# Three quads of expert weights copied during the row scatters, and a first quad of single tiles, in a two-layer mixture-of-experts kernel

## The chip, the core and the metric

The kernel runs on one core of a Trainium2 chip. A core has five engines with a queue each: TensorE (PE in the profile; PEld is its weight loading), VectorE (DVE), ScalarE (ACT), GpSimd (POOL) and SyncE (SP). [...] DMA engines move data between the on-chip memory and DRAM. The metric is the device time of one execution in microseconds.

## The reference

Two layers, each of an attention and a mixture of experts, over x of 8 sequences by 512 tokens by 128 channels. Only the last part, the experts of layer 1, is touched by the steps that follow:

```python
logits = hidden_states @ router_w + router_b
probs = softmax(logits)
topw, topi = top_k(probs, 4)                    # 4 of 16 experts for each token
topw = topw / topw.sum(-1)
combine = sum(one_hot(topi, 16) * topw[..., None], axis=2)
for each expert e:                              # w1: 128 x 256, w2: 256 x 128
    hmid = gelu(x @ w1[e] + b1[e])
    out += (hmid @ w2[e] + b2[e]) * combine[:, e]
```

4096 tokens with four experts each make 16384 assignments. All data is float32.

## The kernel before, in words

The kernel does not multiply every token by every expert. `route1(b)` finds the four experts of each token of sequence b. Its `scatter(t, rw)` then writes each token's row with its weight and its later place (130 numbers) to the DRAM tensor `rows1`, sorted by expert: 128 indirect DMAs of 128 rows (L1532), issued by POOL. While layer 1's attention and routing run, the order on the engines is found by a planner (`Order`) that holds costs and due times; it is the same in both kernels.

After this comes the stage of the expert tiles, whose order is written out by hand under `tc.manual_schedule()`. `plan()` counts the rows of each expert and divides them into tiles of 128 rows that belong to one expert; there are room and loops for 144 tiles, that is `QUADS` = 36 quads of four. For each tile it computes where the rows begin (`of_tile`), where the expert's weights begin (`off1`) and which rows aren't its own (`nowhere`). For a quad q:

- `fetch(q)` reads the four tiles of rows into `de[q]`, three DMAs on SP and one on ACT (L1690). It runs `AHEAD` = 4 quads ahead.
- `prepare(q)` transposes the four tiles on PE (L1696), copies for each tile the expert's weights from `fw1` and `fw2`, which hold all experts, to `w1_ring` and `w2_ring` on DVE (L1701, L1702), and then copies the transposed tiles to `dT` (L1703).
- `first(q)` multiplies by w1 (L1712, two products a tile, each two records in the profile) and applies gelu with the bias on ACT (L1718).
- `second(q)` multiplies by w2 (L1729), sets the places of rows that aren't the tile's own out of bounds (`to`, L1736), multiplies by the weight (y, L1737) and scatters four tiles of results to `res1` by indirect DMAs on POOL (L1739).

The loop overlaps three quads: in turn q stand `prepare(q + 1)`, `first(q)`, `fetch(q + 4)` and `second(q - 1)`. At the end the results are read back, four for each token, and added on DVE (L1772).

The on-chip memory is given out in pools. `stage.close()` releases all pools of layer 1's attention and routing together (`work1`, `small1`, `psum1`), and `work2` with all rings of the expert tiles takes their place. In `work1` lie the tiles of attention as well as `rows`, from which the row scatters read.

Of the kernel before, what the change touches and what calls it, by code (L numbers as in the profile page):

```python
# [9 lines left out]
F32 = mybir.dt.float32  # L10
I32 = mybir.dt.int32
# [3 lines left out]
ALU = mybir.AluOpType  # L15
AX = mybir.AxisListType

P = 128
B = 8
S = 512  # L20
NT = S // P
C = 128
# [15 lines left out]
I1 = 256  # L38
NC1 = I1 // P
WE = I1 + NC1  # L40

W1 = C + 2
WEIGHT, DEST = C, C + 1
REGION = B * S
NA = B * S * K1
QUADS = -(-(NA + E1 * (P - 1)) // (4 * P))
# [143 lines left out]
def two_layers(ctx: ExitStack, tc: tile.TileContext, a: dict, out: bass.AP):  # L190
    nc = tc.nc

    const = ctx.enter_context(tc.tile_pool(name="const", bufs=1))
# [4 lines left out]
    stage = ExitStack()  # L198
    const0 = stage.enter_context(tc.tile_pool(name="const0", bufs=1))

    def ring(pool, n, shape, name, dtype=F32):
        return Ring([pool.tile(shape, dtype, tag=f"{name}{i}", bufs=1, name=f"{name}{i}") for i in range(n)])

    def ring_of(pool, n, shape, name, dtype=F32):
        return [pool.tile(shape, dtype, tag=f"{name}{i}", bufs=1, name=f"{name}{i}") for i in range(n)]
# [19 lines left out]
    ident = const.tile([P, P], F32, name="ident")  # L225
# [61 lines left out]
    work = stage.enter_context(tc.tile_pool(name="work0", bufs=1))  # L287
    small = stage.enter_context(tc.tile_pool(name="small0", bufs=1))
    stage_psum = stage.enter_context(tc.tile_pool(name="psum0", bufs=1, space=bass.MemoryType.PSUM))
    tokens, columns = [P, NT, C], [P, S]  # L290
# [37 lines left out]
    zeros = const.tile([P, S], F32, name="zeros")  # L328
# [35 lines left out]
    v_ring = ring(work, 3, columns, "vT")  # L364
# [73 lines left out]
    def tiled(t2):  # L438
        return t2.rearrange("p (t c) -> p t c", t=NT)
# [20 lines left out]
    def statistics(first, last):  # L460

        yield landing(3.0 + first)
        for b in range(first, last):
            yield DVE, 1.5
            for t in range(NT):
                nc.vector.bn_stats(st_a[:, t, :], xs[b][:, t, :])
                nc.vector.bn_aggr(mv_a[:, b, t, :], st_a[:, t, :])
        yield ACT, 0.6, EXP
        rs, sh = rs_a[:, first:last, :], sh_a[:, first:last, :]
        inverse_root(rs, mv_a[:, first:last, :, 1], bias=eps)  # L470
        yield DVE, 0.2
        nc.vector.scalar_tensor_tensor(sh, mv_a[:, first:last, :, 0], -1.0, rs, ALU.mult, ALU.mult)
        for b in range(first, last):
            have_stats[b].set(order.now)
# [494 lines left out]
    work = stage.enter_context(tc.tile_pool(name="work_e", bufs=1))  # L969
# [63 lines left out]
        nc.scalar.preload_act_table_set(EXP)  # L1033

    stage.close()
    work = stage.enter_context(tc.tile_pool(name="work1", bufs=1))
    small = stage.enter_context(tc.tile_pool(name="small1", bufs=1))


    ng = NH * DK  # L1040
    full = [P, NT, K1, E1]
    ys_ring = ring(work, 2, [P, NT, 2, C], "ys")
    u_ring = ring(work, 4, tokens, "u")
    hn_ring = ring(work, 2, tokens, "hn")
    h1_ring = ring(work, 2, columns, "h1T")
    v_ring = ring(work, 3, columns, "vT")
    gk_ring = ring(work, 2, [ng, S], "gk")
    kq_ring = ring(work, 2, columns, "kq")
    za_ring = ring(work, 2, [ng, S], "za")
    gate_ring = ring(work, 3, columns, "gate")  # L1050

    four = [P, DK, S]
    kb_ring = ring(work, 3, four, "kb")
    gb_both = experts.tile([P, 2, DK, S], F32, tag="first", name="gb_both")
    qb_both = experts.tile([P, 2, DK, S], F32, tag="second", name="qb_both")
    gb_ring = Ring([gb_both[:, i] for i in range(2)])
# [4 lines left out]
    y_ring = ring(work, 2, columns, "yT")  # L1061
# [523 lines left out]
    fw1, fw2 = late  # L1585

    stage.close()
    work = ctx.enter_context(tc.tile_pool(name="work2", bufs=2))


    de_ring = ring_of(work, 8, [P, 4, W1], "de")
    to_ring = ring_of(work, 4, [P, 4], "to", I32)
    w1_ring = ring_of(work, 3, [P, 4, WE], "qw1")
    w2_ring = ring_of(work, 4, [P, 4, I1], "qw2")
    dT_ring = ring_of(work, 3, [P, S], "dT")
    hT_ring = ring_of(work, 3, [P, NC1, S], "qh")
    y_ring = ring_of(work, 4, [P, 4, C], "qy")
    yk_ring = ring_of(work, B, [P, NT, K1, C], "yk")
    psum2 = ctx.enter_context(tc.tile_pool(name="psum2", bufs=1, space=bass.MemoryType.PSUM))
    qT_banks = ring_of(psum2, 2, [P, S], "qT")  # L1600
    mid_banks = ring_of(psum2, 4, [P, S], "mid")
    qy_banks = ring_of(psum2, 2, [P, S], "qyp")
# [14 lines left out]
    nowhere = const.tile([P, 4 * QUADS], I32, name="nowhere")  # L1617
    de, hot_w, cold = {}, {}, {}
# [60 lines left out]
    def value(src, engine, low, high):  # L1679
        return nc.values_load(  # L1680
            src, engines=[engine], min_val=low, max_val=high, skip_runtime_bounds_check_because="clamped in plan()"
        )

    def fetch(q):

        de[q] = de_ring[q % len(de_ring)]
        for engine, queue, tiles_of in ((ET.SP, nc.sync, range(3)), (ET.Activation, nc.scalar, range(3, 4))):
            at = [value(of_tile[0:1, 1, 4 * q + i : 4 * q + i + 1], engine, 0, E1 * REGION - P) for i in tiles_of]
            for i in tiles_of:
                queue.dma_start(de[q][:, i, :], rows1[bass.ds(at[i - tiles_of[0]], P), :])  # L1690

    def prepare(q):

        ps = qT_banks[q % 2]
        for i in range(4):
            nc.tensor.transpose(ps[:, i * P : (i + 1) * P], de[q][:, i, 0:C], ident)  # L1696
        w1_q, w2_q, dT = w1_ring[q % 3], w2_ring[q % 4], dT_ring[q % 3]
        for i in range(4):
            n = 4 * q + i
            at = value(off1[0:1, n : n + 1], ET.DVE, 0, (E1 - 1) * WE)  # L1700
            nc.vector.tensor_copy(w1_q[:, i, :], fw1[:, bass.ds(at, WE)])  # L1701
            nc.vector.tensor_copy(w2_q[:, i, :], fw2[:, bass.ds(at, I1)])  # L1702
        nc.vector.tensor_copy(dT, ps)  # L1703

    def first(q):

        w1_q, dT, hT = w1_ring[q % 3], dT_ring[q % 3], hT_ring[q % 3]
        mid = mid_banks[2 * (q % 2) : 2 * (q % 2) + 2]
        for i in range(4):
            here = slice(i * P, (i + 1) * P)  # L1710
            for c in range(NC1):
                nc.tensor.matmul(  # L1712
                    mid[c][:, here], lhsT=w1_q[:, i, c * P : (c + 1) * P], rhs=dT[:, here], start=True, stop=True
                )
        for i in range(4):
            here = slice(i * P, (i + 1) * P)
            for c in range(NC1):
                nc.scalar.activation(  # L1718
                    hT[:, c, here], mid[c][:, here], AF.Gelu, bias=w1_q[:, i, I1 + c : I1 + c + 1]
                )  # L1720

    def second(q):

        w2_q, hT, to, y = w2_ring[q % 4], hT_ring[q % 3], to_ring[q % 4], y_ring[q % 4]
        ps = qy_banks[q % 2]
        for i in range(4):
            here = slice(i * P, (i + 1) * P)
            for c in range(NC1):
                nc.tensor.matmul(  # L1729
                    ps[:, here],  # L1730
                    lhsT=hT[:, c, here],
                    rhs=w2_q[:, i, c * C : (c + 1) * C],
                    start=c == 0,
                    stop=c == NC1 - 1,
                )
        nc.vector.tensor_tensor(to, de[q][:, :, DEST].bitcast(I32), nowhere[:, 4 * q : 4 * q + 4], ALU.max)  # L1736
        nc.vector.tensor_mul(y, tiled(ps), de[q][:, :, WEIGHT : WEIGHT + 1].to_broadcast([P, 4, C]))  # L1737
        for i in range(4):
            nc.gpsimd.indirect_dma_start(  # L1739
                out=res1_w[4 * q + i],  # L1740
                out_offset=bass.IndirectOffsetOnAxis(ap=to[:, i : i + 1], axis=0),
                in_=y[:, i, :],
                in_offset=None,
                bounds_check=NA - 1,
                oob_is_err=False,
            )

    AHEAD = 4
    with tc.manual_schedule():
        plan()  # L1750
        for q in range(AHEAD):
            fetch(q)
        prepare(0)
        for q in range(QUADS + 1):
            if q + 1 < QUADS:
                prepare(q + 1)
            if q < QUADS:
                first(q)
            if q + AHEAD < QUADS:
                fetch(q + AHEAD)  # L1760
            if q > 0:
                second(q - 1)


        for b in range(B):
            nc.sync.dma_start(
                yk_ring[b].rearrange("p t k c -> p (t k c)"),
                res1[b * S * K1 : (b + 1) * S * K1, :].rearrange("(p n) c -> p (n c)", p=P),
            )
        for b in range(B):  # L1770
            for k in range(K1):
                nc.vector.tensor_add(xs[b], xs[b], yk_ring[b][:, :, k, :])  # L1772
            nc.scalar.dma_start(out[b].rearrange("(t p) c -> p t c", p=P), xs[b])
# [37 lines left out]
```

## Time and profile before

| | us |
|---|---|
| median of three runs | 1123.48 |
| lowest and highest run | 1116.67, 1125.98 |
| the profiled execution's own time | 1110.57 |
| its span, first to last instruction | 1108.8 |
| last row scatter issued (L1532) | 826.0 |
| first, last result scatter issued (L1739) | 844.6, 1075.0 |

The profile is of one execution. Its times are counted from its first instruction. Busy time of the engines over the span: PE 831.4 us (75%), DVE 624.4 (56%), ACT 473.0 (43%), POOL 453.6 (41%). The granted TensorE clock is 0.823 of full speed in the mean; in a stretch it is a mean of pieces at 1.0 and at 0.5. In a timeline row the columns are: start, length, engine, source line, operation, what it writes and reads (buffer numbers left out), how often, and in brackets the idle time of the engine before it with what ended it. "issue" there means that the profile shows nothing that it waited for. In a row of windows they are: the stretch, its length, then busy time and count for PE, PEld, DVE, ACT and POOL, the granted clock, the busy share of the DMA engines and GB/s. In a row of the costliest groups: busy time in all and mean ns of one, then the idle time before them with its main releaser.

### The profile page before, as it was taken

To read this page: it belongs to the slowest core of one execution; us is meant where nothing else is said; L and a number is where in the kernel's file an instruction comes from. 1 tells how busy PE (TensorE), PEld (TensorE's weight loads), DVE (VectorE), ACT (ScalarE), POOL (GpSimd) and SP (SyncE) were. 2 spreads that over 40 slices of the span, in tenths; PEclk is the share of its full clock that TensorE was granted. 3 is DMA by queue.
4 is the path that set the end of the run, shared out by engine and by line. 5 is a ranking of instruction groups with operands and counts; after the bars stand their busy time and mean duration, and the time that the engine had idled before them with its cause. 6 is when DMAs were issued, how large, how long until landed. Compare 5 with 4: busy or idle time off the path is not lost. (4 is left out here: it accounts for less than half of the span.)

```text
span 1108.8 us, 13427 instructions
## 1 busy us (share of the span) xinstructions
PE 831.4 (75%) x3819; PEld 547.1 (49%) x3819; DVE 624.4 (56%) x1592; ACT 473.0 (43%) x1040; POOL 453.6 (41%) x466
## 2 busy tenths in 40 slices
PE   6888998996889299696799687675728677777730
PEld 3544465553445144233476434454418677677630
DVE  5499988778693111255866466362435445455417
ACT  6544656451624044285466654444413233243220
POOL 6200005307454335200035538585553656566650
PEclk9888889869788599898898878686758889988965
DMA  7986667464244300269741065552114232223119
GB/s 177 221 237 146 151 141 193 103 160 109 74 97 147 76 9 20 95 179 233 176 121 46 32 167 155 147 156 73 37 51 106 79 82 82 74 80 87 48 34 357
DMA packets 75531, 131.93 MB, mean 119 GB/s; under 512 B 13044, under 2 KB 54902, under 8 KB 67264
## 3 DMA queue, kind: packets, MB, share of 16 engines
q1 hardware_dynamic: 46400, 91.12, 32.3%
q0 software_dynamic: 14832, 27.84, 8.5%
q10 hardware_dynamic: 14224, 12.11, 3.7%
q8 instruction: 30, 0.49, 0.2%
q14 instruction: 45, 0.37, 0.1%
HBM read 94.79 MB, written 41.14 MB: 123 GB/s over the span
## 5 line engine op out<-in xcount | busy, mean ns | idle before, releaser
L1532 POOL DMA_INDIRECT rows<-rows,si x128 | 152.3, 1190 | 211.6 <-DVE tmp L1502 116.1
L1739 POOL DMA_INDIRECT res<-qy,to x144 | 143.3, 995 | 105.7 <-DVE qw L1701 65.6
L876 POOL DMA_INDIRECT row<-rows,si x64 | 90.1, 1408 | 226.0 <-DVE qT L587 113.7
L1718 ACT ACTIVATE qh<-mid,qw 128x128 f32<-128x128 f32 x288 | 78.7, 391 | 173.3 <-remote 90.8
L1712 PE MATMUL mid<-dT,qw 128*128 128x128 f32 x576 | 89.7, 308 | 39.0 <-issue 23.5
L1712 PEld LDWEIGHTS mid<-dT,qw 128*128 128x128 f32 x576 | 80.7, 218 | 47.9 <-issue 30.7
L671 PE MATMUL acc<-add,center 128*128 128x512 f32 x128 | 76.1, 750 | 16.6 <-DVE add L700 14.4
L1729 PE MATMUL qyp<-qw,qh 128*128 128x128 f32 x576 | 78.6, 294 | 1.6 <-issue 1.5
L1729 PEld LDWEIGHTS qyp<-qw,qh 128*128 128x128 f32 x576 | 75.8, 212 | 1.4 <-issue 1.3
L694 DVE TENSOR_TENSOR_SCAN add<-dec,add 128x2048 f32<-128x2048 f32 x16 | 70.8, 4425 | 0.7
L1737 DVE TENSOR_TENSOR qy<-qyp,de 128x512 f32<-128x512 f32 x36 | 24.8, 688 | 80.3 <-remote 44.9
L179 ACT ACT_TABLE_LOAD x48 | 61.6, 1283 | 5.2 <-issue 3.2
L1701 DVE COPY qw<-fw 128x258 f32 x144 | 43.6, 303 | 28.6 <-issue 12.0
L671 PEld LDWEIGHTS acc<-add,center 128*128 128x128 f32 x128 | 29.7, 243 | 60.0 <-issue 33.8
L1012 POOL DMA_INDIRECT res<-y,de x32 | 31.4, 980 | 46.5 <-DVE dT L985 21.9
L1696 PE MATMUL qT<-ident,de 128*128 128x128 f32 x144 | 26.1, 290 | 24.6 <-DMA de<-rows 14.2
L1317 PE MATMUL acc<-ident,kb 128*128 128x128 f32 x256 | 38.2, 320 | 7.2 <-DVE kb L1307 7.2
L662 ACT ACTIVATE dec<-dec 128x2048 f32<-128x2048 f32 x16 | 30.5, 1908 | 30.6 <-DVE dec L682 30.6
L1702 DVE COPY qw<-fw 128x256 f32 x144 | 42.3, 294 | 2.0 <-DVE qw L1701 1.0
L1317 PEld LDWEIGHTS acc<-ident,kb 128*128 128x128 f32 x256 | 36.9, 234 | 12.1 <-DVE kb L1307 12.0
L789 PE MATMUL bank<-xT,rw 128*128 128x512 f32 x64 | 39.4, 751 | 4.1 <-ACT xT L781 3.6
L952 PE MATMUL idle_bank<-zeros,ident 128*128 128x512 f32 x76 | 40.8, 665 | 0.8 <-DVE y L1006 0.8
(336 smaller groups left out, 1761.7 us busy)
## 6 DMA issues: line engine op xcount, KB each, us to landing
add<-keys SPq DMA_DIRECT2D x16, 1024.0 KB
qb_first<-queries SPq DMA_DIRECT2D x8, 1024.0 KB
qb_second<-queries SPq DMA_DIRECT2D x8, 1024.0 KB
kb<-pairs SPq DMA_DIRECT2D x8, 1024.0 KB
gb_both<-decays SPq DMA_DIRECT2D x8, 1024.0 KB
qb_both<-pairs SPq DMA_DIRECT2D x8, 1024.0 KB
yk<-res SPq DMA_DIRECT2D x8, 1024.0 KB
de<-rows SPq DMA_DIRECT2D x108, 65.0 KB
```

The source lines that it names most:

```text
L179: self.load(table)
L671: nc.tensor.matmul(acc, lhsT=center, rhs=st[:, j, :], start=g + j == 0, stop=(g + 1) * J + j == D + J - 1)
L694: nc.vector.tensor_tensor_scan(flat, dec.rearrange("p j t -> p (j t)"), flat, 0.0, ALU.mult, ALU.add)
L876: nc.gpsimd.indirect_dma_start(out=row0_w[(b * NT + t) * 2 + k], out_offset=bass.IndirectOffsetOnAxis(ap=m.si[:, t, k : k + 1], axis=0), i ...
L1317: nc.tensor.matmul(chunk(acc, t), lhsT=chunk(st[:, j, :], t), rhs=ident, start=j + t == 0, stop=j + t == DK + NT - 2)
L1532: nc.gpsimd.indirect_dma_start(out=rows1_w[(b * NT + t) * K1 + k], out_offset=bass.IndirectOffsetOnAxis(ap=m.si[:, t, k : k + 1], axis=0), ...
L1701: nc.vector.tensor_copy(w1_q[:, i, :], fw1[:, bass.ds(at, WE)])
L1702: nc.vector.tensor_copy(w2_q[:, i, :], fw2[:, bass.ds(at, I1)])
L1712: nc.tensor.matmul(mid[c][:, here], lhsT=w1_q[:, i, c * P : (c + 1) * P], rhs=dT[:, here], start=True, stop=True)
L1718: nc.scalar.activation(hT[:, c, here], mid[c][:, here], AF.Gelu, bias=w1_q[:, i, I1 + c : I1 + c + 1])
L1729: nc.tensor.matmul(ps[:, here], lhsT=hT[:, c, here], rhs=w2_q[:, i, c * C : (c + 1) * C], start=c == 0, stop=c == NC1 - 1,)
L1739: nc.gpsimd.indirect_dma_start(out=res1_w[4 * q + i], out_offset=bass.IndirectOffsetOnAxis(ap=to[:, i : i + 1], axis=0), in_=y[:, i, :], i ...
```

## The change

The rings of layer 1's attention whose last use is early (`hn`, `h1T`, `vT`, `gk`, `kq`, `za`, `kb`) get a pool of their own, `early1`, and the two weight rings of the expert tiles get `early2`, which takes its place. The weight copies leave `prepare` for `weights(q)`; those of quads 0 to 2 stand behind `plan()` and ahead of the fetches, the others at the end of a turn. The loop runs over `units` instead of quads: four single tiles for quad 0, two pairs for quad 1, then whole quads. Unit 0's `first` stands ahead of unit 1's transposes. Six products of constants stand behind `plan()` on PE, then one product that reads `gate`, which POOL sets behind its row scatters, then three more products of constants.

```diff
     stage.close()
+    early_work = stage.enter_context(tc.tile_pool(name="early1", bufs=1))
     work = stage.enter_context(tc.tile_pool(name="work1", bufs=1))
...
-    hn_ring = ring(work, 2, tokens, "hn")
+    hn_ring = ring(early_work, 2, tokens, "hn")
...
-    kb_ring = ring(work, 3, four, "kb")
+    kb_ring = ring(early_work, 3, four, "kb")
...
     stage.close()
+    early_work = ctx.enter_context(tc.tile_pool(name="early2", bufs=1))
     work = ctx.enter_context(tc.tile_pool(name="work2", bufs=2))
...
-    w1_ring = ring_of(work, 3, [P, 4, WE], "qw1")
-    w2_ring = ring_of(work, 4, [P, 4, I1], "qw2")
+    w1_ring = ring_of(early_work, 3, [P, 4, WE], "qw1")
+    w2_ring = ring_of(early_work, 4, [P, 4, I1], "qw2")
...
-    def prepare(q):
-        ps = qT_banks[q % 2]
-        for i in range(4):
-            nc.tensor.transpose(ps[:, i * P : (i + 1) * P], de[q][:, i, 0:C], ident)
-        w1_q, w2_q, dT = w1_ring[q % 3], w2_ring[q % 4], dT_ring[q % 3]
+    def weights(q):
+        w1_q, w2_q = w1_ring[q % 3], w2_ring[q % 4]
         for i in range(4):
             n = 4 * q + i
             at = value(off1[0:1, n : n + 1], ET.DVE, 0, (E1 - 1) * WE)
             nc.vector.tensor_copy(w1_q[:, i, :], fw1[:, bass.ds(at, WE)])
             nc.vector.tensor_copy(w2_q[:, i, :], fw2[:, bass.ds(at, I1)])
-        nc.vector.tensor_copy(dT, ps)
+    units = [(0, range(i, i + 1)) for i in range(4)] + [(1, range(0, 2)), (1, range(2, 4))]
+    units += [(q, range(4)) for q in range(2, QUADS)]
+    def prepare(u):
+        q, tiles_of = units[u]
+        ps, dT = qT_banks[u % 2], dT_ring[u % 3]
+        for i in tiles_of:
+            nc.tensor.transpose(ps[:, i * P : (i + 1) * P], de[q][:, i, 0:C], ident)
+        nc.vector.tensor_copy(dT[:, span(tiles_of)], ps[:, span(tiles_of)])
...
+    def warm(n):
+        for _ in range(n):
+            nc.tensor.matmul(mid_banks[3], lhsT=ident, rhs=zeros, start=True, stop=True)
     AHEAD = 4
+    gate = const.tile([P, 1], F32, name="gate")
     with tc.manual_schedule():
         plan()
+        for q in range(3):
+            weights(q)
+        warm(6)
+        nc.gpsimd.memset(gate, 0.0)
+        nc.tensor.matmul(mid_banks[3][:, 0:1], lhsT=ident, rhs=gate, start=True, stop=True)
+        warm(3)
         for q in range(AHEAD):
             fetch(q)
-        prepare(0)
-        for q in range(QUADS + 1):
-            if q + 1 < QUADS:
-                prepare(q + 1)
-            if q < QUADS:
-                first(q)
-            if q + AHEAD < QUADS:
-                fetch(q + AHEAD)
-            if q > 0:
-                second(q - 1)
+        for u in range(len(units) + 1):
+            here = u < len(units)
+            q = units[u][0] if here else QUADS
+            if u == 0:
+                prepare(0)
+                first(0)
+            if u + 1 < len(units):
+                prepare(u + 1)
+            if u > 0 and here:
+                first(u)
+            if here:
+                if units[u][1][0] == 0 and q + AHEAD < QUADS:
+                    fetch(q + AHEAD)
+            if u > 0:
+                second(u - 1)
+            if here and units[u][1][-1] == 3 and 0 < q < QUADS - 2:
+                weights(q + 2)
```

`span(tiles_of)` is the slice of columns of a unit's tiles. `first(u)` and `second(u)` are as before, but loop over `tiles_of` and take their banks and rings (`dT`, `hT`, `to`, `y`) by u; the weight rings and `de` stay by q.

More of the change, by code (lines that the diff above doesn't have):

```diff
@@ L1043, in two_layers @@
     u_ring = ring(work, 4, tokens, "u")
-    hn_ring = ring(work, 2, tokens, "hn")
[L1045 to L1049, printed above, removed]
+    hn_ring = ring(early_work, 2, tokens, "hn")
+    h1_ring = ring(early_work, 2, columns, "h1T")
+    v_ring = ring(early_work, 3, columns, "vT")
+    gk_ring = ring(early_work, 2, [ng, S], "gk")
+    kq_ring = ring(early_work, 2, columns, "kq")
+    za_ring = ring(early_work, 2, [ng, S], "za")
     gate_ring = ring(work, 3, columns, "gate")
     four = [P, DK, S]
-    kb_ring = ring(work, 3, four, "kb")
+    kb_ring = ring(early_work, 3, four, "kb")
     gb_both = experts.tile([P, 2, DK, S], F32, tag="first", name="gb_both")
@@ L1702, in prepare, with span, first @@
             nc.vector.tensor_copy(w2_q[:, i, :], fw2[:, bass.ds(at, I1)])
[L1703 to L1709, printed above, removed]
+    units = [(0, range(i, i + 1)) for i in range(4)] + [(1, range(0, 2)), (1, range(2, 4))]
+    units += [(q, range(4)) for q in range(2, QUADS)]
+    def span(tiles_of):
+        return slice(tiles_of[0] * P, (tiles_of[-1] + 1) * P)
+    def prepare(u):
[4 more added lines that the diff above has]
+        nc.vector.tensor_copy(dT[:, span(tiles_of)], ps[:, span(tiles_of)])
+    def first(u):
+        q, tiles_of = units[u]
+        w1_q, dT, hT = w1_ring[q % 3], dT_ring[u % 3], hT_ring[u % 3]
+        mid = mid_banks[2 * (u % 2) : 2 * (u % 2) + 2]
+        for i in tiles_of:
             here = slice(i * P, (i + 1) * P)
@@ L1714, in first @@
                 )
-        for i in range(4):
+        for i in tiles_of:
             here = slice(i * P, (i + 1) * P)
@@ L1720, in first, with second @@
                 )
[L1722 to L1726, printed above, removed]
+    def second(u):
+        q, tiles_of = units[u]
+        w2_q, hT, to, y = w2_ring[q % 4], hT_ring[u % 3], to_ring[u % 4], y_ring[u % 4]
+        ps = qy_banks[u % 2]
+        for i in tiles_of:
             here = slice(i * P, (i + 1) * P)
@@ L1735, in second @@
                 )
-        nc.vector.tensor_tensor(to, de[q][:, :, DEST].bitcast(I32), nowhere[:, 4 * q : 4 * q + 4], ALU.max)
-        nc.vector.tensor_mul(y, tiled(ps), de[q][:, :, WEIGHT : WEIGHT + 1].to_broadcast([P, 4, C]))
-        for i in range(4):
+        of = slice(tiles_of[0], tiles_of[-1] + 1)
+        n = len(tiles_of)
+        nc.vector.tensor_tensor(
+            to[:, of], de[q][:, of, DEST].bitcast(I32), nowhere[:, 4 * q + of.start : 4 * q + of.stop], ALU.max
+        )
+        nc.vector.tensor_mul(
+            y[:, of, :],
+            ps[:, span(tiles_of)].rearrange("p (t c) -> p t c", c=C),
+            de[q][:, of, WEIGHT : WEIGHT + 1].to_broadcast([P, n, C]),
+        )
+        for i in tiles_of:
             nc.gpsimd.indirect_dma_start(
```

## The prediction

> **What bounds the kernel now.** I first read the page for the shares, then the timeline around the place of the change (800 to 860 us), then the stage behind it, and last the granted clock. The change touches the expert tiles of layer 1: from the last row scatter of the routing (827 us) to the last result scatter (1076 us), a stage of some 250 us in a span of 1108.8. On the page these two groups carry it:
>
> ```profile
> L1739 POOL DMA_INDIRECT res<-qy,to x144 | 143.3, 995 | 105.7 <-DVE qw L1701 65.6
> ...
> L1712 PE MATMUL mid<-dT,qw 128*128 128x128 f32 x576 | 89.7, 308 | 39.0 <-issue 23.5
> ```
>
> 144 scatters, 36 quads of four tiles, with 105.7 us of idle POOL before them: POOL isn't packed. Back to back, scatters start 1.29 us apart, so a quad would need 5.14 us; the trace has the first scatter at 844.57 and the last at 1075.0, which is 6.43 us for a quad. POOL therefore follows something else, except at the very end, where three quads of scatters stand back to back. Of the POOL idle time one piece is the start. The timeline shows it:
>
> ```profile
> 826.02 0.98 POOL L1532 DMA_INDIRECT rows<-rows,si  x1 [0.30 <-issue]
> 828.88 0.29 DVE L1701 COPY qw<-fw 128x258 f32 x1 [8.89 <-DMA rows<-rows,si]
> 828.92 29.50 SPq L1690 DMA_DIRECT2D de<-rows  x33
> ...
> 831.08 0.45 PE L1696 MATMUL qT<-ident,de 128*128 128x128 f32 x1 [12.11 <-DMA de<-rows]
> ...
> 833.56 0.69 DVE L1703 COPY dT<-qT 128x512 f32<-128x512 f32 x1 [2.18 <-PE qT L1696]
> ...
> 835.48 3.62 PE L1712 MATMUL mid<-dT,qw 128*128 128x128 f32 x16
> ...
> 838.70 1.05 ACT L1718 ACTIVATE qh<-mid,qw 128x128 f32<-128x128 f32 x3 [28.01 <-DMA de<-rows]
> ...
> 841.61 1.95 PE L1729 MATMUL qyp<-qw,qh 128*128 128x128 f32 x16
> ...
> 843.83 1.95 PE L1712 MATMUL mid<-dT,qw 128*128 128x128 f32 x16
> ...
> 844.57 0.98 POOL L1739 DMA_INDIRECT res<-qy,to  x1 [17.56 <-DVE qw L1701]
> ```
>
> The reader is to see three things. The weight copies wait 8.89 us for the row scatters, though they read nothing of them. The fetches start at 828.92 and the first tile reaches PE 2.16 us later. Then a whole quad passes each step before the next begins, so POOL stands still for 17.56 us. PE is at half clock through most of this:
>
> ```profile
> 836.00:839.50 3.50, 3.50 (x18) 3.50 (x18) 2.74 (x11) 0.74 (x3) 0.00 (x0) 0.50 0.39 94
> 839.50:843.00 3.50, 3.50 (x32) 3.50 (x31) 0.76 (x2) 2.96 (x12) 0.00 (x0) 0.94 0.33 78
> ```
>
> PE is busy all through both 3.5 us windows, with 18 matmuls at clock 0.50 and 32 at 0.94. Behind the start the order is PE's: 900 to 920 us holds three quads, 15.7 us of it PE busy, and most of the rest is this:
>
> ```profile
> 905.31 0.61 PE L1712 MATMUL mid<-dT,qw 128*128 128x128 f32 x4
> 906.92 0.27 PE L1712 MATMUL mid<-dT,qw 128*128 128x128 f32 x1 [1.00 <-issue]
> 907.63 0.27 PE L1712 MATMUL mid<-dT,qw 128*128 128x128 f32 x1 [0.44 <-issue]
> 908.35 0.57 PE L1712 MATMUL mid<-dT,qw 128*128 128x128 f32 x1 [0.45 <-issue]
> 909.76 1.03 PE L1712 MATMUL mid<-dT,qw 128*128 128x128 f32 x4 [0.84 <-issue]
> ```
>
> For some 4 us PE issues about one instruction every 0.71 us and waits for nothing that the profile shows. There are eleven such places, halts below, from 862 to 1053 us, of 1.5 to 8 us and mostly 20 us apart.
>
> **The loop behind the start** isn't changed. Before, DVE does copies(q+2), dT(q+2), to(q), y(q) and so on round; after, the copies stand at the end of a turn instead of at the beginning of the next, which is the same ring. PE's order (transposes, first, second) and the 288 copies are the same too. I cost it at 0; DVE's ring isn't covered by anything, but it doesn't get longer.
>
> **Weights copied during the scatters.** Twelve tiles (three quads) at 0.61 us for two copies and a register load (829.27 to 830.89 has a tile every 0.61 us) are 7.3 us. DVE is done with the plan at 819.99 and idle until 828.88, so they end at 827.3, under that idle time and 3.7 us before the first transposed tile needs DVE. What does it bring? In the trace the first quad's copies end at 831.4 and the dT copy still waits for PE until 833.53; the copies were hidden, bar the 0.1 us before the second quad's. So the step itself brings 0 to 0.5 us. If the cover were gone (the own pool not released), dT would come at 828.9 + 7.3 = 836.2.
>
> A rule speaks against it. The Trainium skill, SBUF — State Buffer, section "Who interferes with whom", says that a DVE copy in its two-port mode takes the port pair that GpSimd also uses, and the later one is blocked wholly. By it the 24 copies of 0.29 us could hold up the last scatters by up to 7 us, and the fetches with them. The rows: the 75 result scatters that overlap these very copies by over 0.2 us take 1007 ns in the mean, the others 982. Six scatters stand beside the copies, so 0.15 us by the trace against 7 by the rule. I take 0.2.
>
> **First quad by single tiles, next transpose behind.** Before, `first(0)` stands behind all eight transposes of quads 0 and 1, and so behind quad 1's fetches: 835.48. After, it needs one tile: landed 831.05, transposed 831.4, dT of a quarter width (0.69 us for 512 columns, so some 0.25) by 831.7. Then PE's work up to `first` of quad 2, in full-clock rows: transposes of four quads 4 x 0.60, `first` of two quads 2 x 1.95, `second` of quad 0 and half of quad 1 1.5 x 1.95: 9.2 us, from 831.1 to 840.3. PE can't have it without gaps: tiles of quad 0 arrive until 833.1 and SP issues a quad's fetches every 2.5 us, so quad 3's, which stand in front of `first` of quad 2 as they do now, land at about 840.4 (the last is issued at 838.11, and 2.2 to 2.3 us pass before PE has it). I get 841.1 instead of 843.83: 2.7 us, and half a quad's `second`, 1.0 us, is then already done: **3.7 us**. The added small steps (four more dT copies, to and y each, some 0.2 us apiece on DVE, 2 to 3 us in all) lie beside fetches and PE. The first scatter comes at about 835 instead of 844.57, some 9 us earlier, but POOL then waits for y as it did.
>
> **Nine products and the gate.** In rows of the same shape (L952) a product takes two records of 0.43 us at full clock (0.59 with the drain), 0.85 at half. Starting at 819.0, when the plan leaves PE, six take 5.1 to 10.2 us; the gate waits on POOL for the memset behind the last scatter (827.0), and behind it stand PE's last three and all transposes. At full clock they end at 830.0, before the first tile; wholly at half clock at 834.4, which would hold the transposes up for 3.3 us. The rule in the Trainium skill, TensorE: Matmul & The Clock Gate, section "Part 1: The HAM clock gate", is that some 3.4 us of sustained work lift the clock and an idle window of that length drops it. By it the clock is up from 823 or so and stays up at 831: all of the 3.7. The trace is less kind: PE was busy 2.15 of the 3 us from 797 to 800, and the clock still fell to 0.50 soon after 802. If the sparse first tiles let it fall for one window, single tiles cost twice and 1.5 us is lost: 2.2 left. I take 3.5 us for the whole start, as the row and rule are equally near, less the 0.2 of the scatters, with a few tenths back from the copies. Ends: 0 (products in the way) and 6, since before, y of quad 1 starts at 850.46, 2.9 us behind its products, and that delay may fall elsewhere.
>
> **Other places.** The new pools move tiles of layer 1 to other addresses; its first tiles wait for the same results of layer 0. I cost it at 0, with 1 us either way. At the end, yk loads and adds stay.
>
> **Sum.** Against the profiled execution's own 1110.57 us (span 1108.8): minus 3.5, 1107. The three timed runs have the median 1123.48, 1.2% above the profiled one, from 1116.67 to 1125.98; I move the same 3.5 us over: **1120.0**. A measurement of this kernel can tell about 1%, 11 us, from no change.
>
> **Rivals.**
> 1. POOL is the bound, and all of its earlier start counts: 844.57 - 835.2 = 9.4 us, 1114. For it: the first quads and the last three are packed on POOL. Against: 105.7 us of idle POOL in between. 12%.
> 2. The pool isn't released by itself, and the copies still wait for the row scatters. Then dT of tile 0 comes at 836.2 and `first` of quad 2 some 8.2 us behind, at 844.5, with half a quad more done: 1123. Against: the early pool's tiles are last used by the attention, long before 819. 10%.
> 3. Slower: the halts of PE. Each costs 4 us and about 2 more at half clock behind it (the windows after them show 0.50). The new program has some 40 more PE records, half a quad, and an earlier start of the loop, which gives such halts another phase. From one halt more on the gain is gone: 3.5 - 6, 1126; two are 1132. For it: they stand every 3.1 quads whatever else goes on. Against: nothing in the change adds SP, DVE or PE work to the loop. 18%.
>
> The forecast has 60%. Its own range is 0 to 6 us, 1117 to 1124, plus some 3 us for the measurement. With rival 1 below and rival 3 above I give 1108 to 1129 for 8 in 10. Faster by over 1% needs more than rival 1 gives: 0.10. Slower by over 1% needs two halts more: 0.07. The same: 0.83.
>
> **What would show it.** Right: copies L1701 of three quads between 820 and 828, last row scatter still near 827, PE clock 1.0 at 831, first result scatter at 834 to 837 and `first` of quad 2 near 841; then the same 6.4 us a quad. Wrong: a copy that waits for the row scatters (rival 2); row scatters well over 1.0 us (the port rule); products still running when the first tile has landed; another number of halts, or 5.2 us a quad.

## The result, and the profile after

| | before | after |
|---|---|---|
| median of four runs each, in us | 1124.73 | 1111.5 |
| lowest and highest run | 1116.67, 1126.42 | 1102.78, 1112.38 |
| the profiled execution's own time, and its span | 1110.57, 1108.8 | 1112.12, 1110.1 |
| last row scatter issued | 826.0 | 833.9 |
| first, last result scatter | 844.6, 1075.0 | 843.3, 1076.8 |

The ratio is 0.988, with the interval 0.9836 to 0.9923: 13 us less, where 3.5 were forecast. The two profiled executions say something else: after is 1.6 us longer. Neither can be taken as it stands. The profiled after is 4.3 us late already at the first row scatter of layer 1 (575.9 against 571.6 us), in instructions that both kernels have in the same order, and 7.85 us late at the last one; of the change, only the new addresses reach back there, and e2 below shows nothing from them. And four runs are few: 59 runs of before on one chip lay between 1096.97 and 1118.71. Two longer comparisons, told below, put the change at 0.9945 (0.9908 to 0.9983) and 0.9941 (0.992 to 0.9961): about **6 us less**. The medians alone differ by less, 3.2 us in the first of the two and 5.0 in the second. The 3.5 us of the forecast lie inside the first interval and just outside the second (4.0 to 8.2 us), so the size is known to some 2 us. The two profiles agree once both are counted from the last row scatter, where the stage of the change begins: the last result scatter stands 248.96 us behind it before and 242.91 after, 6.05 us less. Here are the last scatters, before and after:

```profile
1074.99 0.98 POOL L1739 DMA_INDIRECT res<-qy,to  x1 [0.30 <-issue]
```

```profile
1076.78 0.98 POOL L1762 DMA_INDIRECT res<-qy,to  x1 [0.30 <-issue]
```

The groups of after that answer to the two of before, from the page; first busy time and mean ns of one, then the idle time before them:

```profile
L1762 POOL DMA_INDIRECT res<-qy,to x144 | 142.8, 991 | 100.2 <-DVE qw L1700 50.1
...
L1726 PE MATMUL mid<-dT,qw 128*128 128x128 f32 x576 | 88.5, 309 | 35.4 <-issue 26.7
```

POOL has lost 5.5 us of idle time, and is still far from packed. The timeline of after, at the places that the prediction named:

```profile
19.66 0.12 POOL L1783 MEMSET gate<- 128x1 f32 x1
...
828.49 8.10 PE L1774 MATMUL mid<-zeros,ident 128*128 128x512 f32 x12
...
830.26 0.30 DVE L1700 COPY qw<-fw 128x258 f32 x1 [0.69 <-issue]
...
832.50 1.07 POOL L1533 DMA_INDIRECT rows<-rows,si  x1 [0.30 <-issue]
...
833.87 0.98 POOL L1533 DMA_INDIRECT rows<-rows,si  x1 [0.30 <-issue]
...
836.66 13.29 SPq L1692 DMA_DIRECT2D de<-rows  x16
...
839.22 0.27 PE L1715 MATMUL qT<-ident,de 128*128 128x128 f32 x1
...
839.64 0.28 DVE L1701 COPY qw<-fw 128x256 f32 x1
839.97 0.29 DVE L1716 COPY dT<-qT 128x128 f32<-128x128 f32 x1
...
843.29 0.98 POOL L1762 DMA_INDIRECT res<-qy,to  x1 [8.43 <-DVE to L1753]
...
849.35 1.95 PE L1726 MATMUL mid<-dT,qw 128*128 128x128 f32 x16
```

Read it from the bottom. `first` of quad 2 (849.35) stands 15.47 us behind the last row scatter, before 17.81. The first result scatter stands 9.41 behind it, before 18.54. The copies no longer wait for the row scatters; they start once the plan is done, which in this execution is late (829.6), so that the last of them (839.64) ends against the first dT copy. And the first line is a surprise: the memset that should open the gate ran at 19.66 us. In the code it stands behind the row scatters, as the section on the change says; in POOL's order it stands near the beginning.

The clock, in the windows view (stretch, length, busy time and count of PE, PEld, DVE, ACT, POOL, granted clock, DMA share, GB/s):

```profile
829.00:844.00 15.00, 13.73 (x45) 7.03 (x44) 8.67 (x33) 1.65 (x6) 5.37 (x7) 0.84 0.29 76
844.00:860.00 16.00, 16.00 (x144) 15.80 (x143) 10.86 (x38) 8.01 (x29) 8.49 (x10) 1.00 0.44 111
```

In the first stretch the clock is 0.84, where before has 0.64 in the same stretch and 0.50 from 821 to 836 us, which is the same stretch counted from the last row scatter; in the second PE is busy without a gap at full clock. Behind it the halts are there as before. One of them, from the timeline of the same execution:

```profile
886.86 0.27 PE L1715 MATMUL qT<-ident,de 128*128 128x128 f32 x1 [1.16 <-issue]
...
887.31 0.98 POOL L1762 DMA_INDIRECT res<-qy,to  x1 [0.31 <-issue]
...
888.30 0.27 PE L1715 MATMUL qT<-ident,de 128*128 128x128 f32 x1 [1.17 <-issue]
...
891.29 0.98 POOL L1762 DMA_INDIRECT res<-qy,to  x1 [3.01 <-DVE qw L1700]
```

PE takes one instruction in 0.7 or 1.4 us. The end of one of POOL's rows is shown beside it: the halt lies on the end of a row of eight scatters (878.19 to 888.29), and then POOL waits 3.01 us. What that means is shown by e11 below.

### The profile page after: what moved, and what is told of

The parts are those of the page before. It is cut to its first block, busy times and chain, and to the rows that moved or that the text cites. A ratio compares the mean times of both kernels' runs of the same rounds, so it can differ in the third digit from the quotient of the medians.

```text
span 1110.1 us, 13463 instructions
## 1 busy us (share of the span) xinstructions
PE 844.3 (76%) x3839; PEld 556.1 (50%) x3839; DVE 628.3 (57%) x1604; ACT 472.9 (43%) x1040; POOL 453.0 (41%) x467
## 4 chain that ended last, share of the span: by engine, by line
PE 20%; issue 20%; DVE 8%; DMA 7%; POOL 3%; ACT 2%; another core or an unknown queue 2%; SPq 1%; DVEq 1%; POOLq 0%; ACTq 0%
PE mid L1726 6%; PE qyp L1744 5%; DMA qb_both<-pairs 2%; DVE x L1814 2%; POOL res L1012 2%; PE acc L1318 1%; PE qT L1715 1%; DVE kb L1304 1%; DMA decays<-gk 1%; PE acc L1162 1%; PE bank L1284 1%; DMA gb_both<-decays 1%; DVE kb L1308 1%; DVEq L1682 1%
## 5 line engine op out<-in xcount | busy, mean ns | idle before, releaser
L1756 DVE TENSOR_TENSOR qy<-qyp,de 128x512 f32<-128x512 f32 (+2 forms) x40 | 25.4, 635 | 63.8 <-remote 18.8
L1012 POOL DMA_INDIRECT res<-y,de x32 | 31.4, 980 | 44.9 <-DVE y L1006 37.3
L952 PE MATMUL idle_bank<-zeros,ident 128*128 128x512 f32 x76 | 43.6, 704 | 0.8 <-DVE y L1006 0.8
L1318 PEld LDWEIGHTS acc<-ident,kb 128*128 128x128 f32 x256 | 37.3, 236 | 12.6 <-DVE kb L1308 12.1
L1136 DVE BATCH_NORM_STATS2 st<-acc 128x6 f32<-128x128 f32 x64 | 17.5, 273 | 37.9 <-PE acc L1162 22.9
```

The costliest lines, as they stand in the source:

```text
L1012: nc.gpsimd.indirect_dma_start(out=res0_w[e * NT + t], out_offset=bass.IndirectOffsetOnAxis(ap=de0[e][:, t, DEST : DEST + 1].bitcast(I32), ...
L1318: nc.tensor.matmul(chunk(acc, t), lhsT=chunk(st[:, j, :], t), rhs=ident, start=j + t == 0, stop=j + t == DK + NT - 2)
```

## The experiments

Four chips ran them, and each experiment is compared with runs of before on its own chip. Medians of before are given in brackets. On chips A (1109.98 us) and D (1122.81) the kernels' profiles show the halts of the prediction; on B (1021.57) and C (1021.34) they show none. The table counts from SP's first fetch of rows, which leaves out what lay upstream.

| us behind SP's first fetch | first result scatter | `first` of quad 2 | last result scatter |
|---|---|---|---|
| before (first profile) | 15.6 | 14.9 | 246.1 |
| after (first profile) | 6.6 | 12.7 | 240.1 |
| A: e1, after again | 7.2 | 13.3 | 238.2 |
| A: e3, no products | 7.8 | 14.4 | 238.7 |
| C: e9, after again | 7.5 | 13.1 | 196.7 |
| C: e10, pools of before | 12.6 | 18.6 | 202.3 |
| D: e12, more singles | 7.1 | 15.4 | 242.3 |
| D: e11, half of the scatters | 8.3 | 14.2 | 157.2 |

### The size once more, and the parts (chip A)

**e1_after** is the changed kernel without an edit.

> The changed kernel once more, beside the three below. Start theory (the gain is the shorter way from the last row scatter to the steady loop): the stretch from the last row scatter's issue to the last result scatter's issue, 249.0 us in the profile before and 242.9 in the profile after, is 241 to 245 again, and the time is 0.988 to 0.995 of before, since 6 us are 0.5% and the rest of the 13 us was spread of the runs. Halt theory (the loop's halts fall otherwise): the stretch moves by over 3 us from one profile to the next, with no tie to the start. Layout theory (the pools change layer 1's attention): time from the first layer-1 scan to the last row scatter is shorter than before's by several us.

Measured 0.9945 (0.9908 to 0.9983): 6.1 us of 1110, with medians of 1106.82 and 1109.98.

**e2_pools_only** is before with nothing but the two new pools.

```diff
+    early_work = stage.enter_context(tc.tile_pool(name="early1", bufs=1))
...
-    hn_ring = ring(work, 2, tokens, "hn")
+    hn_ring = ring(early_work, 2, tokens, "hn")
...
-    w1_ring = ring_of(work, 3, [P, 4, WE], "qw1")
+    w1_ring = ring_of(early_work, 3, [P, 4, WE], "qw1")
```

> The kernel before with the two new pools alone; loop, order and units as before. Start theory: copies of quad 0 leave the wait for the row scatters, but they were hidden behind fetch and transposes, so 0 to -1 us, ratio 0.998 to 1.002. Layout theory: what the start doesn't explain of the 13 us is here, ratio about 0.994. Halt theory: no change in the order of the loop, so about 1.00.

Measured 0.999 (0.9956 to 1.0023). The new addresses alone do nothing that can be seen; the 13 us of the first comparison were not hidden upstream.

**e3_no_warm** is after without the nine products and the gate.

```diff
-    gate = const.tile([P, 1], F32, name="gate")
...
-        warm(6)
-        nc.gpsimd.memset(gate, 0.0)
-        nc.tensor.matmul(mid_banks[3][:, 0:1], lhsT=ident, rhs=gate, start=True, stop=True)
-        warm(3)
```

> The changed kernel without the nine products of constants and the gated one. Start theory: single tiles at half clock until PE has been busy for a window or two, so 2 to 3 us of the gain are lost: ratio to before 0.993, stretch 245 to 246 us, first result scatter 10.5 to 11.5 us behind the last row scatter (9.4 with the products). Halt theory: 40 PE records fewer, another phase, any value from -4 to +6 us against the changed kernel.

Measured 0.9952 (0.9926 to 0.9978), beside 0.9945 for the whole change. In the table the products bring 0.6 us at the first scatter, 1.1 at `first` of quad 2 and 0.4 at the last scatter. They carry nothing that the comparison can tell from none.

**e4_whole_quads** is after with its first two quads whole.

```diff
-    units = [(0, range(i, i + 1)) for i in range(4)] + [(1, range(0, 2)), (1, range(2, 4))]
-    units += [(q, range(4)) for q in range(2, QUADS)]
+    units = [(q, range(4)) for q in range(QUADS)]
```

> The changed kernel with whole quads as units from the first on; early copies, products and unit 0's first ahead of unit 1's transposes stay. Start theory: first of quad 0 needs all four tiles and PE idles while the first quad's gelu runs; first result scatter 12 to 13 us behind the last row scatter instead of 9.4, first of quad 2 about 1.5 us later; ratio to before 0.992. If POOL's early start were what counts, 3 us of the gain are lost (ratio 0.991).

Measured 0.9993 (0.9968 to 1.0018). Without the single tiles the rest of the change brings nothing that can be seen. Its timeline also shows how the cover of the copies can go:

```profile
806.89 2.07 PE L1130 MATMUL bank<-fb,cT 16*128 16x128 f32 x8 [5.20 <-issue]
...
822.69 0.98 POOL L1533 DMA_INDIRECT rows<-rows,si  x1 [0.30 <-issue]
823.12 0.69 DVE L1519 TENSOR_TENSOR x<-x,bank 128x512 f32<-128x512 f32 x1 [22.61 <-remote]
```

The product ended at 808.96, and the addition that reads it started 14.2 us later, 0.4 us behind the start of the last row scatter. What released it is not known: "remote" in the row stands for another core or an unknown queue. The plan follows that addition, so it ended at 833.9, 1.1 us behind the first fetch at 832.8, and all 24 copies then stood between the plan and the first dT copy. The profiled e2 has the same late addition (plan done at 838.7), the profiled before and after have not; so the start of e2 and e4 is left out of the table, and only their times are used. The profiled e4 is 7.6 us above the median of its 22 runs; how many of the others had the late addition is not known, so what early copies would give to whole quads isn't quite settled.

### Whether the own pool is needed (chips B and C)

**e8_shared_pool** and **e10_shared_pool** are the same kernel: after, with the rings back in the pools of before. The copies stand where after has them, but must wait for the row scatters.

```diff
-    early_work = stage.enter_context(tc.tile_pool(name="early1", bufs=1))
...
-    hn_ring = ring(early_work, 2, tokens, "hn")
+    hn_ring = ring(work, 2, tokens, "hn")
...
-    w1_ring = ring_of(early_work, 3, [P, 4, WE], "qw1")
+    w1_ring = ring_of(work, 3, [P, 4, WE], "qw1")
```

> The changed kernel with the pools of before: the weight rings lie in the common pool again, so the 24 copies of quads 0 to 2 wait for the row scatters and stand in front of the first dT. Rival 2 of the prediction: dT of tile 0 comes 10 us behind the last row scatter instead of 6.1, first result scatter 13 us behind it instead of 9.4 to 10; ratio to before 1.00 (the gain is gone). If the loop behind takes up such a delay: 0.995 as the changed kernel.

> The changed kernel with the pools of before, beside the changed kernel on one chip. Early-copies theory: with copies behind the row scatters the first scatter comes 15 us behind the last row scatter instead of 9.5, and nothing of the gain is left: 0.9995 as in the run before, some 6 us above the changed kernel. If the chip has halts and the loop makes up for a late start: 0.995 to 0.998, within 3 us of the changed kernel.

**e9_after** is after without an edit, beside e10 on chip C.

> The changed kernel again. On the chip of the four runs before this one (before at 1021.6 us), PE has no slow steps and POOL scatters 35 quads back to back at 5.18 us each, while on the chip of the first runs (before at 1110 us) a quad took 6.4 us. If this chip is of the first kind (no halts, POOL the bound), the whole earlier start of the scatters should count: 8 to 10 us, ratio 0.990 to 0.992. If it is of the second kind, the loop takes part of it back: 0.9945 as in the first four runs, within 0.991 to 0.998.

Measured: e8 0.9995 (0.9969 to 1.0021), e10 1.0019 (0.9996 to 1.0041), e9 0.9941 (0.992 to 0.9961). The timeline of e10, from the last row scatter on:

```profile
784.51 0.98 POOL L1532 DMA_INDIRECT rows<-rows,si  x1 [0.30 <-issue]
787.46 0.30 DVE L1698 COPY qw<-fw 128x258 f32 x1 [16.64 <-DMA rows<-rows,si]
...
795.10 0.28 DVE L1714 COPY dT<-qT 128x128 f32<-128x128 f32 x1
...
799.93 0.98 POOL L1760 DMA_INDIRECT res<-qy,to  x1 [14.44 <-DVE to L1751]
```

This is rival 2 in a trace: the copies wait 16.64 us for the row scatters, the first dT copy stands 10.6 us behind the last row scatter (the rival's 836.2 was 10.2 behind), and no gain is left that can be seen. Between e10 and e9 the first scatter moves by 5.1 us and the last by 5.6: on this chip what POOL gains at the start arrives at the end. Of after, e10 keeps the single tiles and the products, so nothing but the two pools lies between the kernels.

### Who sets the loop (chips B and D)

**e5_half_scatters** is after, but from quad 2 on only tiles 0 and 1 of a quad are scattered. The result rows of the other tiles stay at the zeros that a fill in layer 0 sets. The fill is shortened here.

```diff
+        for b in range(2 * B):
+            yield landing(10.0)
+            yield POOL, 1.2
+            nc.gpsimd.dma_start(res1[...], zeros...)
...
+            if q > 1 and i > 1:
+                continue
```

> The changed kernel, in which quads 2 to 35 scatter only two of their four tiles; the result rows of the others are left at zero, which an earlier fill in layer 0 sets, so the output is partial. Measured is the stretch from the first fetch of rows to the last result scatter: 246.1 us in the profile before, 240.1 and 238.3 in two of the changed kernel. If the loop is PE's, as the prediction had it (halts fall on PE whatever POOL does, 19.6 us for three quads), it stays at 230 us or more. If the halts come from scatters that stand back to back (every halt of PE of the profiles ends 0.5 to 0.7 us behind the eighth scatter of a row of eight), there are none left and a quad costs PE's 4.5 to 5.2 us: 175 to 200 us.

Measured 986.6 in one run, beside 1021.57 for before. PE then has a quad in 4.01 us and is busy without a gap from 830 to 930 us, and the last scatter stands 153.5 us behind the first fetch, against 196.7 in e9, the whole kernel on the other chip without halts. So PE alone needs 4.0 us for a quad, and POOL, with 5.14 for four scatters, sets the loop there. The groups of e9, on the other chip without halts, between 845 and 1000 us:

```profile
L1726 PE MATMUL mid<-dT,qw 128*128 128x128 f32 x336 | 42.9, 281 | 17.4 <-DVE dT L1716 17.4
...
L1762 POOL DMA_INDIRECT res<-qy,to x103 | 102.1, 991 | 31.4 <-issue 23.8 <-DMA res<-qy,to 5.2 <-DVE dT L1716 2.1
```

103 scatters with 31.4 us between them is 0.30 us each, the gap of scatters that stand back to back: POOL is packed, and PE is the one that waits. 136 scatters stand in a row there.

**e6_pause_640** and **e7_pause_1280** are after with one more memset on POOL behind the scatters of each quad, of 640 and of 1280 columns.

```diff
+        if tiles_of[-1] == 3:
+            nc.gpsimd.memset(pause, 0.0)
...
+    pause = const.tile([P, 640], F32, name="pause")
```

> The changed kernel with a POOL memset of 640 columns (some 0.6 us by the 0.2 us of the 128-column one) behind each quad's four scatters, 36 in all. Backlog theory (a halt begins when two quads of scatters stand back to back and lasts until POOL is through): the row of eight is broken; if so short a gap is enough, the halts go and POOL sets the pace with 5.14 + 0.9 us a quad: stretch from first fetch to last scatter 225 to 235 us, ratio to before 0.98 to 0.99. If it isn't enough, the halts stay and the memsets come on top: 240 to 255 us, ratio 0.995 to 1.01. If PE halts by itself: no change, 238 to 241.

> As before it, with a memset of 1280 columns (1.1 to 1.3 us). Backlog theory: no two quads within 1.4 us of each other, the halts go or get short; POOL's pace is 5.14 + 1.5 = 6.6 us a quad, as slow as the loop is now: 238 to 246 us, ratio 0.993 to 1.00, with few slow steps on PE. If PE halts by itself: halts stay as many and POOL's longer turn comes into the way at some: 242 to 255 us, ratio over 1.00.

Measured 1.0126 (1.0081 to 1.0171) and 1.0301 (1.0256 to 1.0346). The timeline of e6:

```profile
906.78 0.97 POOL L1762 DMA_INDIRECT res<-qy,to  x1 [0.30 <-issue]
907.74 0.71 POOL L1771 MEMSET pause<- 128x640 f32 x1
908.62 1.02 POOL L1762 DMA_INDIRECT res<-qy,to  x1 [0.17 <-DVE qw L1700]
```

From scatter to scatter it is 1.84 us with the memset, 1.28 without: 0.56 more, 20 us in 36 quads. After itself was not run on chip B; taken at 0.9941, its ratio on chip C, e6 is 19 us longer, and e7 is 37. By this reckoning nearly all of the added POOL time arrives at the end.

**e11_half_scatters** is the kernel of e5 on chip D, where the halts are.

> The changed kernel with two of four scatters left out from quad 2 on (result rows of the other tiles stay at zero, set by a fill in layer 0), for a chip that has halts. On a chip without them a quad cost PE's 4.0 us. If the halts come from scatters that stand back to back, they are gone here too and a quad costs 4.0 to 4.5 us: first fetch to last scatter 150 to 175 us. If they are PE's own on such a chip, whatever POOL does, quads stay near 6 us: over 200 us. On a chip without halts it only repeats 153 us.

Measured 1030.49 in one run, beside 1122.81: 92 us less, where chip B gave 35. The same 150 us, first in e11, then in e12 (told below), which scatters all tiles on the same chip:

```profile
845.00:995.00 150.00, 146.53 (x1289) 144.57 (x1287) 113.17 (x380) 79.03 (x286) 73.68 (x75) 0.99 0.36 91
```

```profile
845.00:995.00 150.00, 115.11 (x871) 109.35 (x869) 80.26 (x271) 52.00 (x190) 89.26 (x90) 0.91 0.33 87
```

PE goes from 871 matmuls in this stretch to 1289 and is hardly ever idle. The halts are gone with half of the scatters. So they do not come from PE's own work, of which e11 does just as much, but hang on POOL's scatters. Whether it is their number or their standing back to back, these runs do not separate: e11 changes both, and e6 and e7, which break up the rows, ran where there are no halts. The timeline of before speaks for the rows. The last scatter of a row of eight stands here among the slow steps:

```profile
926.49 0.31 PE L1696 MATMUL qT<-ident,de 128*128 128x128 f32 x1 [1.11 <-issue]
...
927.00 0.98 POOL L1739 DMA_INDIRECT res<-qy,to  x1 [0.30 <-issue]
927.89 0.40 PE L1712 MATMUL mid<-dT,qw 128*128 128x128 f32 x2 [1.09 <-issue]
929.33 2.09 PE L1712 MATMUL mid<-dT,qw 128*128 128x128 f32 x9 [1.04 <-issue]
...
929.84 0.69 DVE L1737 TENSOR_TENSOR qy<-qyp,de 128x512 f32<-128x512 f32 x1 [3.08 <-remote]
...
930.81 0.98 POOL L1739 DMA_INDIRECT res<-qy,to  x1 [2.82 <-DVE qw L1701]
```

The row ends at 927.98, PE issues back to back again from 929.33, and DVE's y, whose products were done at 924.5, starts at 929.84. Then POOL, which had run dry, goes on. Before has eleven rows of eight or more scatters between 854 and 1052 us, and slow steps (one or two instructions each 0.7 us, or each 1.4) at the end of every one; PE issues back to back again 1.2 to 1.6 us behind it. The eight rows of four behind the first row have none at their ends. Loading of code is not the cause, at least there: from 898 to 912 us, around the halt at 905, the profile has no packet on the queues of instructions.

**e12_more_singles** (chip D) has single tiles for quads 0 and 1 and pairs for quad 2.

```diff
+    units = [(q, range(i, i + 1)) for q in range(2) for i in range(4)] + [(2, range(0, 2)), (2, range(2, 4))]
+    units += [(q, range(4)) for q in range(3, QUADS)]
```

> The changed kernel with quad 1 by single tiles too and quad 2 by two pairs. In the profile of the changed kernel on a chip without halts, POOL idles some 3.5 us between the scatters of quads 0 and 2, because the pairs' y come late. If POOL is the bound from the first scatter on, 1 to 3 us of this are gained: ratio to before 0.991 to 0.993 on a chip without halts (0.9941 for the changed kernel), first fetch to last scatter 194 to 196 us instead of 196.7. On a chip with halts 236 to 240 us and 0.993 to 0.996, within the uncertainty of the changed kernel's 0.9945.

Measured 0.995 (0.9929 to 0.9972), beside e1's 0.9945 on chip A. More single tiles bring no more that can be seen. No kernel tried here beats the change.

## Why the prediction was right, and where it was not

The direction and the range held; the size came out larger. 3.5 us were forecast, and about 6 measured, the upper end of the forecast's own 0 to 6. That the 13 us of the first comparison (1111.5) still lie between 1108 and 1129 is owed to the room left for spread and for rival 1, not to the sum.

- **"What bounds the kernel now."** The step that failed is "POOL therefore follows something else", and behind it "the order is PE's". Idle POOL time, at 6.43 us a quad (6.47, counted between the first scatters of quads 0 and 35), was taken as proof that POOL doesn't set the loop. e11 shows that the halts depend on POOL's scatters: towards the end of eight that stand back to back PE, SP and DVE creep, no y comes, POOL runs dry, and this looks like a POOL that waits for others. Without halts, e9 shows POOL packed outright, and e5, e6 and e7 show the loop getting shorter and longer with POOL's work.
- **"First quad by single tiles".** Its own terms held: `first` of quad 2 comes 2.34 us earlier behind the last row scatter (forecast 2.7), with half a quad's `second` (1.0) done besides. The mis-sized term is the first scatter, 9 us earlier, counted as nothing because "POOL then waits for y as it did". The lead of the first scatter is 9.13 us, that of quad 8's 8.0, of quad 24's 6.72 and of the last 6.05: two thirds of it arrive. Where before had its first row of four scatters, its y of quad 1 started at 850.46, 2.9 us behind its products; the prediction saw that delay and put it into the range only. In after PE has no gap there, and between `first` of quad 2 and `first` of quad 8 it is idle for 5.5 us instead of 9.6. The forecast had nothing for these 4 us, of which some 2 are lost again further on. That the shorter first rows of scatters are what saves them fits e11, but no run singled it out.
- **"Weights copied during the scatters": 0 to 0.5.** Taken alone, nothing speaks against that: e2, where only the first quad's copies are freed of the wait, and e4, where all 24 stand early in the code, gain nothing that can be seen. But it was costed beside the old start. With single tiles and 24 copies in front of the first dT copy the gain hangs on their being early (e9 against e10: 0.9941 and 1.0019). The two steps are no sum: as built here, neither brought anything without the other. What single tiles give with only the first quad's copies in front was not tried.
- **The port rule** of the Trainium skill, SBUF — State Buffer, section "Who interferes with whom", would have cost up to 7 us by the prediction's estimate, the rows gave 0.15. In the first profile two of the row scatters beside the copies took 1.07 us, the rest 0.98 or 0.99, and the starts came at 1.37 instead of 1.29 us: 0.16 us. Only some of the copies stood beside them there. In e9 all 24 do, and of the seven row scatters beside them one took 1.04 us and the others 0.98 or 0.99. The rows were right. The copies lost more: 24 take 9.7 us in the first profile and 8.1 in e9 instead of the 7.3 worked out, and single ones 0.53 and 0.57 us.
- **"Nine products and the gate."** The six took 8.10 us, inside the 5.1 to 10.2 of the forecast, and the clock was 1.00 from 836 to 840 us, as the first tile came, as the rule of the Trainium skill, TensorE: Matmul & The Clock Gate, section "Part 1: The HAM clock gate", had it. But the step that the gate holds the last three until 827.0 was wrong: the memset had run long before, so nothing was held. In the first profile this didn't matter, since the late plan put the products right before the first tile. In e9 the plan was done at 765.2, the products at 775.4, PE then stood idle for 7.74 us, and the windows show the clock down as the first tiles come, as the same rule has it:

```profile
780.00:784.00 4.00, 0.48 (x2) 0.22 (x2) 0.29 (x1) 0.00 (x0) 0.00 (x0) 0.56 0.35 73
```

  e9 gains its 0.6% with the first tiles at half clock, so the 1.5 us at stake were no large part of it. A gate that holds was not tried.
- **"The loop behind the start" and "Other places"** were 0. For the addresses e2 (0.999) agrees. The loop from quad 8's first scatter to the last one takes 178.5 us in after and 176.6 in before: it gains nothing and loses 2 us of the lead.
- **The rivals.** Rival 2 is what e8 and e10 built on purpose, and with its time. Rival 1 had the right engine, with 9.4 us where about 6 arrive: its argument against it, "105.7 us of idle POOL", was the same misreading. Rival 3, one halt more, didn't come: rows of eight scatters and slow steps behind them stand in after much as before (eleven such rows each), and its reason, that halts fall on PE "whatever else goes on", is what e11 refutes.

What stays open: why two chips have no halts at all with the same scatters back to back (136 in a row in e9), by what means scatters make the other engines' steps slow, and why the first comparison gave 13 us. The spread of single runs (1096.97 to 1118.71 for before on chip A) may be the reason for the last, but no run here singled it out.

## What to carry to other kernels

An engine that is idle for more than a third of a stage may still set it: look at what the engines that it waits for were doing while it was last busy, and take away half of its work before deciding. Steps that start the same pipeline need not add up; cost each with the other done and with the other not. A gate is worth what its own record says: find the instruction that opens it in the trace, and read when it ran.

## What was not expected of the hardware

- On two of four chips PE, SP and DVE go at one instruction per 0.7 us or so towards the end of a row of eight or more indirect scatters that stand back to back, and PE is back at pace only 1.2 to 1.6 us behind the end of the row; with half of the scatters left out, two in a row instead of eight, this is gone, and the stage falls from 242 us (e12, same chip) to 157 (e11).
- In e4's profile a DVE addition started 14.2 us after the product that it reads had ended, with no releaser that the profile can name; row scatters stood back to back all that time, and the plan behind it ended 14 us later than in before (833.9 against 820.0).
- The same kernel, before, takes 1110 and 1123 us on the two chips with halts and 1021 on the two without: some 9%, more than ten times what the change is worth. Most of it lies where POOL scatters: between the profiles of e1 and e9, the same kernel on chips A and C, 38 of 96 us fall between the first and the last row scatter, and 42 between that and the last result scatter.
